# Message passing on a graph: more rows fetched by SyncE, and gates by tanh in PSUM

## The chip, the cores and the metric

The kernel runs on one core of one Trainium2 chip. The metric is the device time of one execution in microseconds. The core has five engines with queues of their own: TensorE (PE; its weight loads are listed as PEld), VectorE (DVE), ScalarE (ACT), GpSimd (POOL) and SyncE (SP), which computes nothing and issues DMAs. "PEq", "SPq" and so on are the sequencers, where waits and DMA issues happen.

## What is computed

One layer of an equivariant graph network, with a residual and a layer norm. There are 12500 nodes with 160 features each (64 scalars and 32 vectors of 3) and 400000 edges, sorted by their destination `dst`; `src` is random. Cut to what matters:

```python
h   = lin1(x) * a                                   # per node: 64 scalars, 32 x 3
w   = silu(edge_scalars @ fc_w1) @ fc_w2            # per edge: 224 weights
es, ev = h_s[src], h_v[src]                         # the gather: one row of 160 per edge
mid = products of w, es, ev and edge_attr           # per edge
agg = segment_sum(mid, dst) / 4                     # per node
pre = (self connection of x + agg @ lin2) * a       # 96 scalars, 32 x 3
y   = concat(silu(pre_s[:64]), sigmoid(pre_s[64:96])[:, None] * pre_v)
out = layernorm(x + y)
```

The node attribute `a` scales `pre` as a whole, so silu(z) = z * sigmoid(z) with z = a * pre, and the vectors' gate is sigmoid(a * pre_s[64:96]).

## The kernel before, in words

**Prologue** (lines 203 to 413). The node table `h_tab` (12500 rows of 160 floats, 640 bytes) is made and written to HBM. Weights, indices and constants are loaded. `at` holds the node attribute by tile of 128 nodes.

**Steps** (lines 862 to 908). The edges are cut into 3125 tiles of 128. A step takes a *quad*, four tiles; there are 782 steps. The order of all engines' instructions is written out by hand (`tc.manual_schedule`): each engine runs its instructions in the order in which this loop emits them. Step n emits:

- `fetch(n + 4)`: DMAs on SyncE, the `es` chunk (the edge scalars, two DMAs of 384 KB, once in six steps, two buffers; L200) and indices and edge attributes (L156, L157).
- `fetch_rows(n)` (L735 to L746): see below.
- the gather (L452 to L459): one indirect DMA on GpSimd per tile into `hg`, four buffers of a quad each; or, if the quad is one of `own`, the buffer `hq` that SyncE has filled.
- `weights` (L490): four matmuls from `hid` into `pw` in PSUM, two buffers.
- `turning.pop(0)()`: a tile of nodes, if one is due; what it returns runs on VectorE after the first product (`first`, L884).
- `one_hot` (L561), `products` (L508, and L516 three times) and `select_quad` (L570) on VectorE.
- `add`s into the node sums `acc` (L609), then a later stage of a node job (`step_on`).
- `sum_up`: for the quad two steps back, matmuls `sel`^T x `pr` into `pa` (L577), and when a block is complete its copy on ScalarE (L790).
- `hide(n + 2)`: once in two steps, the hidden layer (L447 on TensorE, Silu on ScalarE, L449), from `es`.
- `output`, `turn_blocks`: the maps of sixteen finished blocks (L601) and the transposes of one pair of blocks (L586). They, the hidden layer, the self connection (L770) and the node tiles share two PSUM banks, `misc`, in turn.

**Rows by SyncE.** `own` (L461) is every 68th step from 76 on that holds a whole quad: 11 quads. For the quad of step m, `places` (L465) loads its 512 indices, at step m-74; `tensor_scalar_mul` on VectorE (L741) turns them to byte offsets at step m-66, two steps behind the own quad before. The fetch is cut into 32 jobs of 16 rows (L479 to L486): one register load of 16 offsets (L480), and 16 DMAs of 640 bytes (L485). A job is emitted on each step whose number is even. The buffer `hq` is single, and SyncE's queue runs in order: its `es` loads, index loads, node loads `xt` (L625) and output stores (L677) stand between the jobs.

**Node jobs** (`finish`, L612 to L680). When the sums of four tiles of 128 nodes are complete, a job is begun (`begin`, L852): its `xt` rows are loaded, and its stages follow one per step. Four `turn`s: two transposes of `acc` into a `misc` bank (L636), which VectorE scales by `at` into `z` (L637). Then `gates`: one Sigmoid over the four tiles on ScalarE (L643). `gated`: two products per tile (L648, L649). `residual`: the addition of `xt` (L657). `moments` (L662, L664), `root` (Sqrt on ScalarE, L668), `norm` (L672, L674) and the store of the output by SyncE (L677). The last job, four tiles of which one is part filled, runs all its stages behind the last step; there `spans` lets each product take all four tiles at once.

Of the kernel before, what the change touches and what calls it, by code (L numbers as in the profile page):

```python
# [10 lines left out]
F32 = mybir.dt.float32  # L11
# [4 lines left out]
AF = mybir.ActivationFunctionType  # L16
OP = mybir.AluOpType
# [4 lines left out]
P = 128  # L22
S = 64
V = 32
V3 = 3 * V
D = S + V3
# [9 lines left out]
CT = 2 * SIDE  # L36
AHEAD = 3 * CT
NF = 4
OWN = 68
BATCH = 16  # L40
EVERY = 2

MARGIN = 128
NO = 16
# [13 lines left out]
def gnn_kernel(  # L58
# [21 lines left out]
    nc = tc.nc  # L80
    N = x.shape[0]
    NT = attr.shape[1]
# [8 lines left out]
    consts = ctx.enter_context(tc.tile_pool(name="consts", bufs=1))  # L91
# [100 lines left out]
    def load_chunk(c, queue=nc.sync):  # L192
        if c in ess:
            return
        t0, halves = chunks[c]
        es = ess[c] = loads.tile([2 * S, SIDE * P], F32, name="es")
        for half, n in enumerate(halves):
            to = es[half * S:(half + 1) * S]
            e0 = (t0 + half * halves[0]) * P
            queue.dma_start(to[:, :n * P], es_t[:, e0:e0 + n * P])  # L200


    ident = consts.tile([P, P], F32, name="ident")
# [24 lines left out]
    with tc.tile_pool(name="nodes", bufs=len(starts)) as nodes, tc.tile_pool(  # L228
        name="nodes_ps", bufs=6, space=PSUM
# [22 lines left out]
        at = consts.tile([P, NT], F32, name="at")  # L252
# [60 lines left out]
        for c0, cn, quarters, cq, xa, xz in loaded:  # L313
# [3 lines left out]
            nt = -(-cn // P)  # L317
            first = c0 // P
            full = cn // P
            for t0 in range(0, nt, U):  # L320
                ps = nps.tile([P, U, P], F32, name="hp")
                for t in range(t0, min(t0 + U, nt)):
                    n = min(P, cn - t * P)
                    nc.tensor.matmul(ps[:n, t - t0], xa[:, t * P:t * P + n], l1,
                                     start=True, stop=True)
                k = min(U, full - t0)
# [3 lines left out]
                if t0 + k < nt <= t0 + U:  # L330
                    n = cn - full * P
# [6 lines left out]
            for u in range(-(-cq // P)):  # L338
                n = min(P, cq - u * P)
# [10 lines left out]
            if cn > full * P:  # L350
                n = cn - full * P
# [7 lines left out]

    load_chunk(0, nc.gpsimd)  # L360
    nc.gpsimd.dma_start(dt, dst)
    iota = consts.tile([P, W], F32, name="iota")
    nc.vector.tensor_copy(iota, iota_i)
    for half in range(2):
# [22 lines left out]
    for to, part, pieces, w, r0, c0, by in maps:  # L387
        for k, piece in enumerate(pieces):
# [3 lines left out]
            m = terms.setdefault((to, part, four), len(terms))  # L392
# [20 lines left out]
    acc = sums.tile([V3, 2, NP], F32, name="acc")  # L413
# [46 lines left out]

    own = [n for n in range(OWN + 8, len(steps) - 4, OWN) if len(steps[n][2]) == Q]  # L461
    by_bytes = h_tab.rearrange("n d -> (n d)").bitcast(U8)
    row_bytes = 4 * D

    def places(pool, n):  # L465

        at_bytes = pool.tile([Q, P], I32, name="at_bytes")
        for k, (t, _, _) in enumerate(steps[n][2]):
            g, u = divmod(t, GT)
            with nc.allow_non_contiguous_dma(reason="the indices of one tile"):  # L470
                nc.sync.dma_start(at_bytes[k:k + 1], src[g][:, u:u + 1].rearrange("p u -> u p"))
        return at_bytes

    def rows_of(pool, at_bytes):

        hq = pool.tile([P, Q, D], F32, name="hq", bufs=1)
        flat_hq = hq.rearrange("p t d -> p (t d)").bitcast(U8)

        def job(t, p0):  # L479
            _, values = nc.values_load_multi_w_load_instructions(  # L480
                at_bytes[t:t + 1, p0:p0 + BATCH], engines=[ENG.SP], min_val=0,
                max_val=(N - 1) * row_bytes,
                skip_runtime_bounds_check_because="every entry of src is the index of a node")
            for p, v in enumerate(values, p0):
                nc.sync.dma_start(flat_hq[p:p + 1, t * row_bytes:(t + 1) * row_bytes],  # L485
                                  by_bytes[ds(v, row_bytes)][None])  # L486

        return hq, [lambda t=t, p0=p0: job(t, p0) for t in range(Q) for p0 in range(0, P, BATCH)]
# [123 lines left out]
    def finish(fin, psum, t0, nt, p, most=NF):  # L612


        whole = nt if p == P else nt - 1
        spans = [(0, nt)] if t0 + nt == tiles_of_nodes else [(k, k + 1) for k in range(nt)]
        xt = fin.tile([P, most, D], F32, name="xt", bufs=2)
        held = []
        if whole < nt:
            nc.vector.memset(xt[:, whole], 0.0)  # L620
        parts = [(slice(t0 * P, (t0 + whole) * P), slice(0, whole), P)] if whole else []
        if whole < nt:
            parts.append((slice((t0 + whole) * P, (t0 + whole) * P + p), slice(whole, nt), p))
        for nodes_of, k, n in parts:
            nc.sync.dma_start(xt[:n, k], x[nodes_of, :].rearrange("(t p) d -> p t d", p=n))  # L625

        def turn(k):
            if not held:
                held.extend(fin.tile([P, most, *shape], F32, name=name) for name, shape in (
                    ("z", [2 * V3]), ("sg", [V3]), ("y", [D]), ("st", [6]), ("mv", [2]),  # L630
                    ("rs", [])))
            z = held[0]
            c = (t0 + k) * P
            pp = psum.tile([P, 2, V3], F32, name="pp", tag="misc")
            for m in range(2):
                nc.tensor.transpose(pp[:, m], acc[:, m, c:c + P], ident[:V3, :V3])  # L636
            return lambda: nc.vector.tensor_scalar(  # L637
                z[:, k], pp.rearrange("p m c -> p (m c)"), at[:, t0 + k:t0 + k + 1], None,
                op0=OP.mult)

        def gates():
            z, sg = held[:2]
            nc.scalar.activation(sg[:, :nt], z[:, :nt, :V3], AF.Sigmoid)  # L643

        def gated():
            z, sg, y = held[:3]
            for k, m in spans:
                nc.vector.tensor_mul(y[:, k:m, :S], z[:, k:m, :S], sg[:, k:m, :S])  # L648
                nc.vector.tensor_mul(  # L649
                    y[:, k:m, S:].rearrange("p t (c i) -> p t i c", i=3),  # L650
                    z[:, k:m, V3:].rearrange("p t (i c) -> p t i c", i=3),
                    sg[:, k:m, None, S:].to_broadcast([P, m - k, 3, V]))

        def residual():
            y = held[2]
            for k, m in spans:
                nc.vector.tensor_add(y[:, k:m], y[:, k:m], xt[:, k:m])  # L657

        def moments():
            _, _, y, st, mv, _ = held  # L660
            for k in range(nt):
                nc.vector.bn_stats(st[:, k], y[:, k])  # L662
            for k in range(nt):
                nc.vector.bn_aggr(mv[:, k], st[:, k])  # L664

        def root():
            mv, rs = held[4:]
            nc.scalar.activation(rs[:, :nt], mv[:, :nt, 1], AF.Sqrt, bias=eps)  # L668

        def norm():  # L670
            _, _, y, _, mv, rs = held
            nc.vector.reciprocal(rs[:, :nt], rs[:, :nt])  # L672
            for k in range(nt):
                nc.vector.tensor_scalar(y[:, k], y[:, k], mv[:, k, 0:1], rs[:, k:k + 1],  # L674
                                        op0=OP.subtract, op1=OP.mult)
            for nodes_of, k, n in parts:
                nc.sync.dma_start(out[nodes_of, :].rearrange("(t p) d -> p t d", p=n), y[:n, k])  # L677

        return [lambda k=k: turn(k) for k in range(nt)] + [
            gates, gated, residual, moments, root, norm]  # L680


    tiles_of_nodes = -(-N // P)
# [5 lines left out]
    with tc.tile_pool(  # L689
        name="fin", bufs=1  # L690
    ) as fin, tc.tile_pool(
        name="mine", bufs=2
    ) as mine, tc.tile_pool(
        name="late", bufs=2
    ) as late, tc.tile_pool(name="edge", bufs=2) as edge, tc.tile_pool(
        name="deep", bufs=4
# [36 lines left out]
        at_of, hq_of, rows_due = {}, {}, []  # L733

        def fetch_rows(n):  # L735

            for m in own:
                if n == max(1, m - OWN - 6):
                    at_of[m] = places(mine, m)
                if n == m - OWN + 2:  # L740
                    nc.vector.tensor_scalar_mul(at_of[m], at_of[m], float(row_bytes))  # L741
                    hq_of[m], jobs = rows_of(mine, at_of[m])
                    rows_due.extend((m, job) for job in jobs)
            if n % EVERY == 0 and rows_due:
                rows_due.pop(0)[1]()
            assert all(m > n for m, _ in rows_due)  # L746

# [114 lines left out]
        with tc.manual_schedule(engines={ENG.PE, ENG.DVE, ENG.Activation, ENG.Pool, ENG.SP}):  # L862
# [6 lines left out]
            for n, (c, i, tiles) in enumerate(steps):  # L869
# [3 lines left out]
                if n in checks:  # L873
                    checks[n]()
                fetch(n + 4)
                fetch_rows(n)
                hg = hq_of.pop(n) if n in own else gather(deep, [index(t) for t, _, _ in tiles])
                pw = weights(pw_ps, hids[c, i // 2], [(half, u - i // 2 * 4) for _, half, u in tiles])
# [62 lines left out]
        with tc.For_i(0, n_redo, 1):  # L941
# [9 lines left out]
            with tc.For_i(0, n_again, 1) as g, tc.For_i(0, GT, 1) as k:  # L951
                t = g * GT + k
# [12 lines left out]
                for k, op in enumerate((OP.min, OP.max)):  # L965
# [14 lines left out]
                                        op1=OP.mult)  # L980
# [69 lines left out]
```

## Time and profile before

| what | value |
|---|---|
| median of 10 runs | 3971.7 us (3969.57 to 3973.46) |
| profiled execution | 3970.37 us |
| its span | 3968.4 us |
| mean granted TensorE clock | 0.971 |
| gathers on GpSimd | 3081 |
| row fetches on SyncE | 5632 |
| Silu, Sigmoid and Sqrt table loads on ScalarE | 48, 25, 25, of 1.283 us each |
| DMA traffic | 412.51 MB, mean 104 GB/s |

The profile is of one execution. A line of its groups gives source line, engine, operation, "out<-in" by the program's names, shapes and count; then busy time and the mean of one in ns; then the idle time of the engine just before them, and what ended most of it. "issue" means that the engine waited for nothing that the profile shows. In a list of waits, a line reads: who waited, for what, total us, times, longest. A timeline lists start, duration, engine, line, operation and count, with adjoining instructions merged. A line of one source line's instructions gives count, minimum, median and maximum in ns, and the first and last start in us. Instructions of SyncE are never counted as busy; its queue is seen in timelines and waits alone.

### The profile page before, as it was taken

How to read it: one execution, taken by the hardware profiler on the slowest of the kernel's cores; microseconds unless marked ns; L12 is line 12 of the kernel's file. 1: busy time of each engine (PE TensorE's matmuls, PEld its weight loads, DVE VectorE, ACT ScalarE, POOL GpSimd, SP SyncE). 2: the span in 40 equal slices, each digit the busy share in tenths (PEclk: the TensorE clock that was granted, in tenths of full speed). 3: DMA queues.
4: the chain of work that ended last, by engine and by line, in shares of the span. 5: the costliest groups of instructions: out<-in, count | busy, mean ns of one | idle time of the engine just before them, and what ended most of it. 6: DMA issues, size and time to landing. Idle time of an engine off the chain costs nothing. (4 is left out here: it accounts for less than half of the span.)

```text
span 3968.4 us, 58310 instructions
## 1 busy us (share of the span) xinstructions
PE 3649.9 (92%) x14291; PEld 1585.7 (40%) x14291; DVE 2416.6 (61%) x6607; ACT 939.9 (24%) x2463; POOL 2946.3 (74%) x3100
## 2 busy tenths in 40 slices
PE   5999999998999999999999999999999999999997
PEld 4343343343444344334334344344343344343343
DVE  5656665655665665656656556656665665665665
ACT  1322221221222222212212222222222222222222
POOL 4777777777777777777777777777777777777774
PEclk8999999999999999999999999999999999999998
DMA  8343444344434344343443433433434444334332
GB/s 231 96 107 86 109 102 105 98 103 105 100 98 109 96 102 105 101 109 89 107 112 90 105 99 99 108 99 96 111 99 107 99 103 105 98 99 108 99 95 67
DMA packets 243271, 412.51 MB, mean 104 GB/s; under 512 B 83147, under 2 KB 173575, under 8 KB 242023
## 3 DMA queue, kind: packets, MB, share of 16 engines
q0 software_dynamic: 150160, 262.93, 25.4%
q1 hardware_dynamic: 92246, 145.66, 15.5%
q8 instruction: 115, 1.88, 0.2%
q14 instruction: 236, 1.93, 0.2%
q10 hardware_dynamic: 514, 0.10, 0.0%
HBM read 392.43 MB, written 16.00 MB: 103 GB/s over the span
## 5 line engine op out<-in xcount | busy, mean ns | idle before, releaser
L456 POOL DMA_INDIRECT hg<-h_tab,idx x3081 | 2932.1, 952 | 946.0 <-issue 850.9
L498 PE MATMUL pw<-w,hid 128*128 128x448 f32 x3126 | 1368.1, 561 | 168.6 <-DVE sel L570 127.6
L577 PE MATMUL pa<-pr,sel 128*64 128x416 f32 x6250 | 1291.8, 535 | 0.0
L516 DVE TENSOR_TENSOR pr<-pw,hg 128x384 f32<-128x384 f32 x2313 | 1137.8, 548 | 0.0
L508 DVE TENSOR_TENSOR pr<-pw,hg 128x512 f32<-128x512 f32 x771 | 532.9, 691 | 933.3 <-DMA hg<-h_tab,idx 669.7
L498 PEld LDWEIGHTS pw<-w,hid 128*128 128x128 f32 x3126 | 555.2, 194 | 649.5 <-issue 453.1
L577 PEld LDWEIGHTS pa<-pr,sel 128*64 128x64 f32 x6250 | 385.9, 138 | 806.1 <-issue 795.3
L790 ACT COPY sa<-pa 128x416 f32<-128x416 f32 x521 | 263.1, 505 | 1366.5 <-PE pa L577 1361.3
L561 DVE TENSOR_TENSOR pw<-rel,iota 128x64 f32<-128x64 int16 x782 | 179.8, 230 | 511.0 <-PE pw L498 506.8
L447 PE MATMUL misc<-es,w 128*128 128x512 f32 (+1 forms) x784 | 445.2, 650 | 22.4 <-DMA es<-in_es_t_dram 19.6
L449 ACT ACTIVATE hid<-misc 128x512 f32<-128x512 f32 x392 | 233.5, 596 | 714.8 <-PE misc L447 714.3
L586 PEld LDWEIGHTS misc<-ident,sa 128*128 128x128 f32 x2084 | 239.5, 141 | 332.5 <-issue 250.7
L601 PE MATMUL misc<-tt,l 128*96 128x256 f32 (+5 forms) x1496 | 349.0, 381 | 13.5 <-DVE z L637 12.0
L586 PE MATMUL misc<-ident,sa 128*128 128x128 f32 x2084 | 329.6, 281 | 20.5 <-DVE z L637 10.6
L570 DVE TENSOR_TENSOR sel<-pw,eas 128x256 f32<-128x256 f32 x782 | 324.4, 415 | 0.0
L589 ACT COPY tt<-misc 128x192 f32<-128x192 f32 x521 | 164.6, 316 | 537.3 <-PE misc L586 522.8
L601 PEld LDWEIGHTS misc<-tt,l 128*96 128x96 f32 (+1 forms) x1496 | 229.0, 164 | 151.8 <-issue 73.0
L447 PEld LDWEIGHTS misc<-es,w 128*128 128x128 f32 x784 | 118.5, 190 | 283.9 <-issue 224.6
L609 DVE TENSOR_TENSOR acc<-acc,os 96x32 f32 x1042 | 195.2, 187 | 23.8 <-ACT os L604 5.5
L591 ACT COPY tt<-misc 128x64 f32<-128x64 f32 x521 | 117.1, 225 | 0.0
L604 ACT COPY os<-misc 96x512 f32<-96x512 f32 (+2 forms) x68 | 38.3, 563 | 316.6 <-PE misc L601 309.2
L636 PE MATMUL misc<-ident,acc 96*128 96x96 f32 x196 | 35.1, 264 | 49.3 <-DVE pw L561 30.8
(87 smaller groups left out, 680.6 us busy)
## 6 DMA issues: line engine op xcount, KB each, us to landing
es<-in_es_t_dram SPq DMA_DIRECT2D x258, 384.0 KB
hq<-h_tab SPq DMA_DIRECT2D x5632, 0.6 KB
hg<-h_tab,idx POOLq DMA_INDIRECT x3081
h_tab<-ht POOLq DMA_DIRECT2D x6, 1280.0 KB
xt<-in_x_dram SPq DMA_DIRECT2D x23, 320.0 KB
out_dram<-y SPq DMA_DIRECT2D x23, 320.0 KB
xv<-in_xv_t_dram SPq DMA_DIRECT2D x25, 187.5 KB
xs<-in_xs_t_dram SPq DMA_DIRECT2D x25, 125.0 KB
```

Of the source, the lines that this page charges most:

```text
L447: nc.tensor.matmul(ph[:k, c], w1[:k, :k], es[:k, t0 * P + c0 * P:t0 * P + c1 * P], start=True, stop=True)
L449: nc.scalar.activation(hid[:k, c], ph[:k, c], AF.Silu, scale=1.0 / math.sqrt(64))
L456: nc.gpsimd.indirect_dma_start(out=hg[:, t, :], out_offset=None, in_=h_tab, in_offset=bass.IndirectOffsetOnAxis(ap=i, axis=0))
L498: nc.tensor.matmul(pw[:, t:t + m, :NWT], hid[:m * S, c * P:(c + 1) * P], w2[:m * S, :m], start=True, stop=True)
L508: nc.vector.tensor_mul(two, pw[:, :n, :2 * S].rearrange("p t (k c) -> p t k c", k=2), hg[:, :n, None, :S].to_broadcast([P, n, 2, S]))
L516: nc.vector.tensor_mul(pr[:, :n, first:first + V3].rearrange("p t (i c) -> p t i c", i=3), pw[:, :n, None, 2 * S + k * V:2 * S + (k + 1) * ...
L570: nc.vector.tensor_mul(sel[:, :n], oh[:, :, None, :].to_broadcast([P, n, 4, W]), by_slot(tiles[0][0])[:, u:u + n, :, None].to_broadcast([P ...
L577: nc.tensor.matmul(pa[half * ROWS:(half + 1) * ROWS, :NPR], sel[:, t].rearrange("p k w -> p (k w)"), pr, start=start, stop=stop)
L586: nc.tensor.transpose(pt[:, four * P:four * P + k], sa[:k, c:c + P], ident[:k, :k])
L601: nc.tensor.matmul(po[:, k, :nb], l2[r, terms[to, part, four]], a[:, :nb], start=(n == 0), stop=(n == len(of) - 1))
L609: nc.vector.tensor_add(window, window, os[:, :, b])
L790: nc.scalar.copy(sa, pas.pop(j)[:, :NPR])
```

## The change

Three constants and the node jobs are changed.

- `OWN` is 48 instead of 68, so `own` is steps 56, 104, ... 776: 16 quads. `places` comes at step m-54 and the scaling at step m-46, still two steps behind the own quad before.
- A job of 16 rows is emitted on the steps whose number is not a multiple of 4, three of four, instead of on every second.
- The gates use sigmoid(z) = (1 + tanh(z/2)) / 2. A constant `half_at` holds at/2. In `turn`, the two transposes go to one stretch of a `misc` bank; ScalarE takes tanh of the scalars' half from PSUM, scaled by `half_at`, into `g`. The function that runs after the first product is three VectorE instructions per tile: (g + 1) * pre for the 64 scalars and for the 96 vector components, both from PSUM into free columns of the same bank, and that times `half_at` plus `xt` into `y`. The stages `gates`, `gated` and `residual`, the tiles `z` and `sg`, and `spans` go. A job has four `turn`s, `moments`, `root` and `norm`: seven steps instead of ten.

```diff
-OWN = 68
+OWN = 48
 BATCH = 16
-EVERY = 2
+EVERY = 4
...
+    half_at = consts.tile([P, NT], F32, name="half_at")
+    nc.vector.tensor_scalar_mul(half_at, at, 0.5)
...
-            z = held[0]
+            g, y = held[:2]
             c = (t0 + k) * P
-            pp = psum.tile([P, 2, V3], F32, name="pp", tag="misc")
+            pp = psum.tile([P, 512], F32, name="pp", tag="misc")
             for m in range(2):
-                nc.tensor.transpose(pp[:, m], acc[:, m, c:c + P], ident[:V3, :V3])
-            return lambda: nc.vector.tensor_scalar(
-                z[:, k], pp.rearrange("p m c -> p (m c)"), at[:, t0 + k:t0 + k + 1], None,
-                op0=OP.mult)
-
-        def gates():
...
-        def gated():
...
-        def residual():
...
+                nc.tensor.transpose(pp[:, m * V3:(m + 1) * V3], acc[:, m, c:c + P], ident[:V3, :V3])
+            half = half_at[:, t0 + k:t0 + k + 1]
+            nc.scalar.activation(g[:, k], pp[:, :V3], AF.Tanh, scale=half)
+            pg = pp[:, 2 * V3:2 * V3 + D]
+
+            def gate():
+                nc.vector.scalar_tensor_tensor(pg[:, :S], g[:, k, :S], 1.0, pp[:, :S],
+                                               op0=OP.add, op1=OP.mult)
+                nc.vector.scalar_tensor_tensor(
+                    pg[:, S:].rearrange("p (c i) -> p i c", i=3),
+                    g[:, k, None, S:].to_broadcast([P, 3, V]), 1.0,
+                    pp[:, V3:2 * V3].rearrange("p (i c) -> p i c", i=3),
+                    op0=OP.add, op1=OP.mult)
+                nc.vector.scalar_tensor_tensor(y[:, k], pg, half, xt[:, k],
+                                               op0=OP.mult, op1=OP.add)
+
+            return gate
...
         return [lambda k=k: turn(k) for k in range(nt)] + [
-            gates, gated, residual, moments, root, norm]
+            moments, root, norm]
...
-            if n % EVERY == 0 and rows_due:
+            if n % EVERY and rows_due:
                 rows_due.pop(0)[1]()
```

More of the change, by code (lines that the diff above doesn't have):

```diff
@@ L615, in finish @@
         whole = nt if p == P else nt - 1
-        spans = [(0, nt)] if t0 + nt == tiles_of_nodes else [(k, k + 1) for k in range(nt)]
         xt = fin.tile([P, most, D], F32, name="xt", bufs=2)
@@ L629, in turn @@
                 held.extend(fin.tile([P, most, *shape], F32, name=name) for name, shape in (
-                    ("z", [2 * V3]), ("sg", [V3]), ("y", [D]), ("st", [6]), ("mv", [2]),
-                    ("rs", [])))
-            z = held[0]
+                    ("g", [V3]), ("y", [D]), ("st", [6]), ("mv", [2]), ("rs", [])))
+            g, y = held[:2]
             c = (t0 + k) * P
-            pp = psum.tile([P, 2, V3], F32, name="pp", tag="misc")
+            pp = psum.tile([P, 512], F32, name="pp", tag="misc")
@@ L635, in turn @@
             for m in range(2):
-                nc.tensor.transpose(pp[:, m], acc[:, m, c:c + P], ident[:V3, :V3])
-            return lambda: nc.vector.tensor_scalar(
-                z[:, k], pp.rearrange("p m c -> p (m c)"), at[:, t0 + k:t0 + k + 1], None,
-                op0=OP.mult)
-        def gates():
-            z, sg = held[:2]
-            nc.scalar.activation(sg[:, :nt], z[:, :nt, :V3], AF.Sigmoid)
-        def gated():
[L646 to L652, printed above, removed]
@@ L654, in residual @@
-        def residual():
-            y = held[2]
-            for k, m in spans:
-                nc.vector.tensor_add(y[:, k:m], y[:, k:m], xt[:, k:m])
+                nc.tensor.transpose(pp[:, m * V3:(m + 1) * V3], acc[:, m, c:c + P], ident[:V3, :V3])
[12 more added lines that the diff above has]
+                                               op0=OP.mult, op1=OP.add)
@@ L659, in moments @@
+            return gate
         def moments():
-            _, _, y, st, mv, _ = held
+            _, y, st, mv, _ = held
             for k in range(nt):
@@ L666, in root @@
         def root():
-            mv, rs = held[4:]
+            mv, rs = held[3:]
             nc.scalar.activation(rs[:, :nt], mv[:, :nt, 1], AF.Sqrt, bias=eps)
         def norm():
-            _, _, y, _, mv, rs = held
+            _, y, _, mv, rs = held
             nc.vector.reciprocal(rs[:, :nt], rs[:, :nt])
```

## The prediction

> **What bounds the kernel now.** I read the page first, then the list of waits, then the timeline of GpSimd, and last the timeline and the waits of SyncE's queue. The page:
>
> ```profile
> PE 3649.9 (92%) x14291; PEld 1585.7 (40%) x14291; DVE 2416.6 (61%) x6607; ACT 939.9 (24%) x2463; POOL 2946.3 (74%) x3100
> L456 POOL DMA_INDIRECT hg<-h_tab,idx x3081 | 2932.1, 952 | 946.0 <-issue 850.9
> L508 DVE TENSOR_TENSOR pr<-pw,hg 128x512 f32<-128x512 f32 x771 | 532.9, 691 | 933.3 <-DMA hg<-h_tab,idx 669.7
> ```
>
> TensorE shows the largest share, but the second line decides. A gather takes 0.952 us, and 850.9 us of the 946.0 us of idle time ahead of gathers is "issue": nothing held them. The third line shows the first product of each step waiting 669.7 us for the gathered rows. GpSimd's timeline, first and last gather:
>
> ```profile
> 61.44 1.04 POOL L456 DMA_INDIRECT hg<-h_tab,idx  x1 [7.28 <-issue]
> ...
> 3931.31 0.95 POOL L456 DMA_INDIRECT hg<-h_tab,idx  x1 [0.31 <-issue]
> ```
>
> From 61.44 to 3932.26 us there are 3081 gathers, 1.256 us each, without a hole. Nearly all else is slack: GpSimd sets the pace, 4 x 1.253 = 5.01 us per step of four tiles. A quad that SyncE fetches spares GpSimd four gathers. That is why SyncE's queue is the second thing to read. Its instructions are not counted as busy on the page, so its load has to be taken from its own rows.
>
> ```profile
> L480 SPq TENSOR_LOAD <-at_bytes x352: 982/1232/1893, 117.0 to 3785.2; - x176
> L485 SPq DMA_DIRECT2D hq<-h_tab x5632: 219/228/312, 118.3 to 3792.5; - x195
> ```
>
> ```profile
> 2309.42 0.41 SPq L677 DMA_DIRECT2D out_dram<-y  x1
> 2309.93 1.13 SPq L200 DMA_DIRECT2D es<-in_es_t_dram  x2
> 2312.63 20.75 SPq L485 DMA_DIRECT2D hq<-h_tab  x48
> 2333.48 1.11 SPq L200 DMA_DIRECT2D es<-in_es_t_dram  x2
> 2336.16 19.73 SPq L485 DMA_DIRECT2D hq<-h_tab  x48
> ```
>
> ```profile
> SPq L677 <- DVE pw L561: 60.8, 2, 35.0
> SPq L485 <- DMA es<-in_es_t_dram: 14.6, 12, 1.9
> ```
>
> The second fence is the timeline of SyncE's queue: three batches of 16 rows take about 20 us, and one `es` load with three batches 23.5 us (2309.93 to 2333.48). The third is what that queue waited for from 2142 to 2458 us, the window in which the quad of step 484 is fetched. It waited 60.8 us at two output stores (it had run ahead of VectorE) and 14.6 us behind `es` transfers: a row's DMA is held until the load ahead of it has drained.
>
> **The SyncE part, step by step.** Before, own quads are steps 76, 144, ... 756: 11. After, 56, 104, ... 776: 16. So 5 x 4 = 20 gathers go, 20 x 1.256 = 25.1 us of GpSimd, and 2560 row fetches come.
>
> *What a fetch costs SyncE.* A batch alone is one register load, 1.23 us and its gap, and 16 rows in 5.12 us: 6.45 us, 206 us for the 32 of a quad. Top down, with everything that the queue carries: from the first load at about 2142.2 to the last row at 2457.9 us is 315.7 us; less the 60.8 us at output stores and 2.1 us of waits for a free `es` buffer leaves 252.8 us of work. This covers 62 steps with ten pairs of `es` loads. After, the 32 batches lie in 42 steps (three of four, from step m-46 to m-5, for own step m), with seven pairs. Three pairs at 1.27 us of issue and some 1.5 us of wait go, 8.3 us, and a third of the index, edge and node transfers, 3 us. So W = 252.8 - 8.3 - 3 = 241.5 us.
>
> *When it may begin and must end.* The first register load waits for VectorE's scaling of the indices (L741), which stands two steps behind the last own quad; the buffer `hq` is single. VectorE's timeline around step 416 prices this:
>
> ```profile
> 2135.01 0.69 DVE L508 TENSOR_TENSOR pr<-pw,hq 128x512 f32<-128x512 f32 x1
> 2139.14 0.69 DVE L508 TENSOR_TENSOR pr<-pw,hg 128x512 f32<-128x512 f32 x1
> 2141.79 0.29 DVE L741 TENSOR_SCALAR at_bytes<-at_bytes 4x128 int32<-4x128 int32 x1
> ```
>
> From the own quad's product to the scaling is 6.8 us. Then 0.3 us to the load, W, and about 2 us until the last rows are there (the shortest time from a gather's end to the product that uses it is 1.7 us; I found no row for a single row's landing). GpSimd's cycle for 48 steps is 47 x 5.01 = 235.6 us; SyncE's is 6.8 + 0.3 + 241.5 + 2 = 250.6 us. SyncE is 15 us too slow, and **it becomes the bound**. Before, the same two sums were 67 x 5.01 = 336 us for GpSimd and 262 us for SyncE.
>
> *What is queued behind it.* SyncE runs behind the steps inside a window, so the output stores no longer hold it (the 60.8 us vanish because they were slack), but the `es` loads come late: in order behind the batches, they feed TensorE's L447. The last load of a window is issued at step m-6, followed by two batches and the index loads, 16 us, and 2 us of landing: the rows are there 18 us after it. The load itself takes about 6 us (the batch held behind it starts again 5 to 6 us after it) and 1.1 us of matmul, and then come some 3.5 steps at the 4.0 us that steps 416 to 421 took when nothing held them (2135.01 to 2155.03 for five), 14 us, and 2 us to the product: 23 us. So up to 5 us more; bounds 0 (if TensorE catches up faster) and 7. I take 5: a cycle of 255.6 us.
>
> *A page that speaks otherwise.* The row says 1.232 us for a register load. The Trainium skill, "DMA: Bandwidth & Descriptors", section "Latency and other measured facts", puts the floor of such a load at about 600 ns. By it W would be 20 us less, the cycle 235 us, and the time GpSimd's own, about 3945 us; the row decides, since no load in the trace is under 0.98 us.
>
> **The gates.** Per tile, the scaling from PSUM (408 ns, L637), two products (215 and 281 ns) and the residual (316 ns) go, 1.22 us, and three instructions with a PSUM operand come. The trace has none of that kind; from the PSUM products of 384 and 512 columns (547, 691 ns) they would take 0.71 us in all, by three times the scaling's row 1.22 us. VectorE gains 0 to 0.5 us a tile, 0 to 50 us over 98 tiles; it has 39% idle, so I count nothing. ScalarE gets 98 tanh of 225 to 316 ns (L591, L589) for 25 sigmoids of 523 ns. Table loads are 1.283 us; 25 for sigmoid go; tanh needs none if it lies in Silu's table, and up to 98, with Silu's reloads, if it does not. ScalarE is 76% idle; at worst the gate, and the products queued behind it, wait 1.28 us in 98 steps, 126 us that lie beside SyncE's longer work. The misc bank is held until the third instruction, about 0.7 us longer; TensorE now waits 58 us behind L637, and that may grow by half, unseen. The residual now needs `xt` one step after its load is issued, not six: VectorE waits there for SyncE to come up, but SyncE's own work is no longer for it, so I count 0, with 8 us x 24 jobs as the other end. Behind the last step the four scalings, gate, products and residual last from 3948.25 to 3952.49 us; four tiles of three instructions take about as long: 0, give or take 1 us.
>
> **The sum.** First register load at 117.0 us as now; first own product at 117 + 241.5 + 2 + 5 = 365.5; fifteen cycles of 255.6, 3834, bring step 776 to 4199.5. Before, from the last own product (3815.0 us, step 756) to the end of the span is 153.4 us; with 20 fewer steps of 5.0 us, 53.4. Span 4253; the profiled execution took 3970.4 for a span of 3968.4, so 2 more: **4255 us**. Its sum is against 3970.4, which lies 1.3 us under the median of 3971.7.
>
> **Rivals.**
> - *GpSimd stays the bound* (ends on the other side). Decided at W = 226.5 us, where SyncE's cycle is 235.6. For it: 206 us of bare batches, 9 of bare `es` issues and some 11 of the other transfers come to 226 us. Against it: the 14.6 us behind `es` in one window. Price: 3970.4 - 25.1 = 3945 us. Chance 0.1, and 0.02 for a cycle that lands within 0.2% of now.
> - *SyncE bounds, but holds behind `es` and late `es` cost nothing*, since compute waits in any case: cycle 255.6 - 10.5 - 5 = 240 to 245, 4005 to 4085. Chance 0.18.
> - *SyncE bounds as summed*, cycle 249 to 261: 4150 to 4340. Chance 0.62.
> - *The gates add to it*: `xt` late by 8 us in 24 jobs, or table loads that lengthen the stretch from own quad to scaling: 4255 + 190 = 4445. Chance 0.08.
>
> That the change does not take effect is excluded: steps and batches follow from the constants. The range leaves out the first and last: 4040 to 4345. A difference of 0.2% (8 us) is about what can be told here: faster 0.1, same 0.02, slower 0.88.
>
> **What would show it.** Right: GpSimd's gathers show waits of several us before step 104 and every 48th step; the product at own steps waits for `hq`; SyncE's waits at L677 shrink to a few us; L447 waits for `es`. Wrong: gathers at 1.253 us without a hole, rows of the last batch landed before their step, or a window's W below 230 us.

## The result and the profile after

The changed kernel takes **4281.12 us** (median of 8 runs, 4274.31 to 4285.45) against 3970.71 us for the kernel before (28 runs beside it): a ratio of 1.078 [1.077, 1.0789], 7.8% slower. The forecast was 4255 us, its range 4040 to 4345. The profiled execution has a span of 4276.3 us at a mean granted TensorE clock of 0.934 (before 3968.4 at 0.971). Line numbers of the kernel after lie a little lower or higher: the gather is L458, SyncE's register load L482, its row DMA L487, the hidden matmul L449, the gates L638 to L649, the output store L672, the scaling of the indices L736.

The page of the kernel after, first the busy times, then three of its groups:

```profile
PE 3718.4 (87%) x14291; PEld 1635.5 (38%) x14291; DVE 2442.9 (57%) x6524; ACT 899.5 (21%) x2488; POOL 2910.4 (68%) x3080
L458 POOL DMA_INDIRECT hg<-h_tab,idx x3061 | 2896.1, 946 | 1278.7 <-issue 849.4
L449 PE MATMUL misc<-es,w 128*128 128x512 f32 (+1 forms) x784 | 494.4, 716 | 398.6 <-DMA es<-in_es_t_dram 373.4
L510 DVE TENSOR_TENSOR pr<-pw,hg 128x512 f32<-128x512 f32 x766 | 529.1, 691 | 158.0 <-DMA hg<-h_tab,idx 100.9
```

Every engine's share has fallen: the bound is none of the five that the page counts as busy. GpSimd did 20 gathers fewer, 25 us, but its idle time ahead of gathers rose from 946.0 to 1278.7 us while "issue" stayed at 849.4. The first product now waits 100.9 us for gathered rows instead of 669.7: the gathers are no longer late. TensorE, which waited little for `es`, waits 373.4 us. The kernel after in the list of waits:

```profile
PE misc L449 <- DMA es<-in_es_t_dram: 373.4, 76, 13.1
POOL hg L458 <- DMA hq<-h_tab: 198.9, 31, 12.8
POOL hg L458 <- DVE pr L518: 136.6, 84, 5.8
DVE y L649 <- DMA xt<-in_x_dram: 103.6, 15, 10.9
```

and what SyncE's own queue waited for:

```profile
SPq L482 <- DVE pw L563: 210.9, 14, 18.9
SPq L487 <- DMA es<-in_es_t_dram: 124.2, 121, 2.1
SPq L672 <- DVE y L669: 29.5, 1, 29.5
```

Everything that waits in the first list waits for a load of SyncE's queue or for a product (L518). The queue itself (second list) waits for VectorE for long only between windows (L482, the first register load, 14 times); a *window* is the stretch from the first register load of an own quad to its last row. Its waits at the output store are one of 29.5 us and one of 18.2, both behind the last window; before they were 556.3 us in 21. The line that puts 198.9 us on `hq` names the wrong load. A gather does not read `hq`, and 33 of the 93 holes in GpSimd's work (212 of the 340 us by which they exceed the usual 0.3 us between gathers) end at a semaphore whose last DMA was an index load. Such a place, in the timelines of SyncE and of GpSimd:

```profile
2344.82 10.51 SPq L487 DMA_DIRECT2D hq<-h_tab  x29
2355.43 1.12 SPq L200 DMA_DIRECT2D es<-in_es_t_dram  x2
2356.86 0.37 SPq L156 DMA_DIRECT2D idx<-in_src_dram  x1
```

```profile
2353.48 0.94 POOL L458 DMA_INDIRECT hg<-h_tab,idx  x1 [0.30 <-issue]
2362.49 0.94 POOL L458 DMA_INDIRECT hg<-h_tab,idx  x1 [8.07 <-DMA hq<-h_tab]
```

GpSimd stands still for 8.07 us until the index load issued at 2356.86 us has landed. That load stood behind rows. And the end of a window, step 440, in the timelines of SyncE and VectorE:

```profile
2395.01 10.42 SPq L487 DMA_DIRECT2D hq<-h_tab  x28
2405.52 1.15 SPq L200 DMA_DIRECT2D es<-in_es_t_dram  x2
```

```profile
2413.95 0.23 DVE L563 TENSOR_TENSOR pw<-rel,iota 128x64 f32<-128x64 int16 x1 [0.83 <-PE pw L500]
...
2417.61 0.69 DVE L510 TENSOR_TENSOR pr<-pw,hq 128x512 f32<-128x512 f32 x1 [0.17 <-DVE pw L563]
...
2424.74 0.21 DVE L736 TENSOR_SCALAR at_bytes<-at_bytes 4x128 int32<-4x128 int32 x1
```

The last row goes out at 2405.4 us, the own quad's product starts 12.2 us later, and 7.1 us after that start the scaling lets the next window begin. The product waited for the weights `pw` (TensorE), not for `hq`; in no window of this run does an own quad's first product wait for `hq`.

The SyncE part of the span, by the prediction's own terms (from the rows of VectorE and SyncE; means over the windows):

| term | predicted | measured |
|---|---|---|
| first own product | 365.5 | 360.4 |
| own product to scaling, and to the first load | 6.8 + 0.3 | 7.1 + 0.3 |
| W, SyncE's work in a window | 241.5 | 239.7 (237.9 to 242.4) |
| last row to own product | 2 + 5 | 9.9 (5.5 to 13.7) |
| cycle of 48 steps | 255.6 | 257.3 |
| last own product to the end of the span | 53.4 | 56.5 |
| span | 4253 | 360.4 + 15 x 257.3 + 56.5 = 4276 |

### The profile page after: what moved, and what is told of

Its sections match the earlier page's. It is cut to its first block, busy times and chain, and to the rows that moved or that the text cites. A ratio compares the mean times of both kernels' runs of the same rounds, so it can differ in the third digit from the quotient of the medians.

```text
span 4276.3 us, 63629 instructions
## 1 busy us (share of the span) xinstructions
PE 3718.4 (87%) x14291; PEld 1635.5 (38%) x14291; DVE 2442.9 (57%) x6524; ACT 899.5 (21%) x2488; POOL 2910.4 (68%) x3080
## 5 line engine op out<-in xcount | busy, mean ns | idle before, releaser
L458 POOL DMA_INDIRECT hg<-h_tab,idx x3061 | 2896.1, 946 | 1278.7 <-issue 849.4
L518 DVE TENSOR_TENSOR pr<-pw,hg 128x384 f32<-128x384 f32 x2298 | 1130.2, 547 | 0.0
L563 DVE TENSOR_TENSOR pw<-rel,iota 128x64 f32<-128x64 int16 x782 | 183.2, 234 | 1445.1 <-PE pw L500 1444.2
L449 PE MATMUL misc<-es,w 128*128 128x512 f32 (+1 forms) x784 | 494.4, 716 | 398.6 <-DMA es<-in_es_t_dram 373.4
L500 PEld LDWEIGHTS pw<-w,hid 128*128 128x128 f32 x3126 | 569.3, 198 | 495.3 <-issue 464.8
L510 DVE TENSOR_TENSOR pr<-pw,hg 128x512 f32<-128x512 f32 x766 | 529.1, 691 | 158.0 <-DMA hg<-h_tab,idx 100.9
L603 PE MATMUL misc<-tt,l 128*96 128x256 f32 (+5 forms) x1496 | 384.2, 409 | 1.5 <-ACT tt L593 1.5
L449 PEld LDWEIGHTS misc<-es,w 128*128 128x128 f32 x784 | 128.3, 205 | 660.7 <-issue 577.2
L603 PEld LDWEIGHTS misc<-tt,l 128*96 128x96 f32 (+1 forms) x1496 | 253.5, 180 | 164.1 <-issue 92.7
L611 DVE TENSOR_TENSOR acc<-acc,os 96x32 f32 x1042 | 194.4, 187 | 25.1 <-ACT os L606 6.9
L649 DVE SCALAR_TENSOR_TENSOR y<-misc,half_at,xt 128x160 f32<-128x160 f32 x98 | 37.6, 384 | 106.5 <-DMA xt<-in_x_dram 103.6
```

The costliest lines, as they stand in the source:

```text
L449: nc.tensor.matmul(ph[:k, c], w1[:k, :k], es[:k, t0 * P + c0 * P:t0 * P + c1 * P], start=True, stop=True)
L458: nc.gpsimd.indirect_dma_start(out=hg[:, t, :], out_offset=None, in_=h_tab, in_offset=bass.IndirectOffsetOnAxis(ap=i, axis=0))
L500: nc.tensor.matmul(pw[:, t:t + m, :NWT], hid[:m * S, c * P:(c + 1) * P], w2[:m * S, :m], start=True, stop=True)
L510: nc.vector.tensor_mul(two, pw[:, :n, :2 * S].rearrange("p t (k c) -> p t k c", k=2), hg[:, :n, None, :S].to_broadcast([P, n, 2, S]))
L518: nc.vector.tensor_mul(pr[:, :n, first:first + V3].rearrange("p t (i c) -> p t i c", i=3), pw[:, :n, None, 2 * S + k * V:2 * S + (k + 1) * ...
L603: nc.tensor.matmul(po[:, k, :nb], l2[r, terms[to, part, four]], a[:, :nb], start=(n == 0), stop=(n == len(of) - 1))
```

## The experiments

Seven runs, e1 to h1, told in a group at the end, were made where the kernel before itself took 5250 to 5340 us; the others were made where it took 3972 to 3975 us, as for the result. A ratio is always to runs of the kernel before at the same place and time, and what the two kinds of places give is not mixed.

**k1: the changed kernel as it is**, beside the next one.

> The changed kernel itself, unaltered, as the control for the kernels beside it. On a chip where the kernel before takes 3971 us: 4281 again, ratio 1.078. On one where it takes 5300 us: SyncE's work per window was 353 us there with the old gates (6185 us, ratio 1.163); the same within 1%, ratio 1.155 to 1.175 (theory A; the gates add at most the 0.3% that they cost alone). Rival B would have it 0.02 or more above the 1.163 of the constants alone.

4282.24 us against 3971.88, 1.078 [1.0762, 1.0798], as expected; W 237.8 to 241.9 us. It stands for the changed kernel in what follows.

**m1: the gates alone.** The constants are those of before, the gates and node jobs those of after.

```diff
-OWN = 48
+OWN = 68
-EVERY = 4
+EVERY = 2
-            if n % EVERY and rows_due:
+            if n % EVERY == 0 and rows_due:
```

> The changed kernel with the two constants put back: the gates alone, on a chip where the kernel before takes 3972 and the changed one 4282 us. Theory A: GpSimd stays the bound with 3081 gathers; VectorE's and ScalarE's savings lie beside it: 3971 us, give or take 5 (1.003 was measured where all queues ran slowly). Rival B (the wait for xt, 103.6 us in the changed kernel, and the bank held longer cost time by themselves): 4030 us or more, with holes between gathers.

3961.71 us (3957.99 to 3964.05) against 3975.47: 0.9966 [0.9954, 0.9978]. The expected 3971, give or take 5, was missed: the gates, which I had counted at nothing, make the kernel 13.8 us *faster*, and the loss of the change lies in its constants: 4281 - 3962, some 320 us. (The constants alone were not run where the kernel before takes 3972 us; this is a difference.) Where the 13.8 us come from is seen in the rows of the gathers from 400 to 3900 us, first of before, then of m1:

```profile
L456 POOL DMA_INDIRECT hg<-h_tab,idx x2787: 942/946/2307, 399.5 to 3900.0; - x200
```

```profile
L458 POOL DMA_INDIRECT hg<-h_tab,idx x2798: 942/946/1098, 399.5 to 3899.6; - x200
```

The median is the same, 946 ns, but the longest was 2307 ns and is 1098. Before, 25 gathers took over 1.1 us, 14.8 us in excess of 946 ns each; in m1 three do, 0.9 us, all in the prologue. Of the 25, four lie in the prologue and 21 lie beside L648, L649 or L657, the products and the residual of a node job. GpSimd's and VectorE's timelines of before:

```profile
2129.57 1.80 POOL L456 DMA_INDIRECT hg<-h_tab,idx  x1 [0.30 <-issue]
...
2134.18 1.61 POOL L456 DMA_INDIRECT hg<-h_tab,idx  x1 [0.30 <-issue]
```

```profile
2129.57 0.21 DVE L648 TENSOR_TENSOR y<-z,sg 128x64 f32<-128x64 f32 x1
2129.70 0.28 DVE L649 TENSOR_TENSOR y<-z,sg 128x96 f32<-128x96 f32 x1
...
2133.81 1.02 DVE L657 TENSOR_TENSOR y<-y,xt 128x160 f32<-128x160 f32 x4
```

The gather that begins amid the run of products takes 1.80 us, the one that begins amid the four additions 1.61 us. These VectorE instructions read both operands from SBUF. In m1 one operand of each lies in PSUM, and no gather that begins beside them is stretched. The products of the steps (L508, L516) have one operand in PSUM as well, and gathers beside them take 0.95 us. The additions into `acc` (L611 in m1), 187 ns each with both operands in SBUF, are still there: of 124 gathers that begin while one runs, 16 take 50 to 152 ns longer. This is what the Trainium skill, "SBUF — State Buffer", section "Who interferes with whom", states: a VectorE instruction with two SBUF inputs contends with a GpSimd instruction that reads SBUF. The page has no price for a gather; here the excess is 0.2 to 1.4 us for each of the 21. The profiled executions differ by 12.4 us of span: 14.7 us less in gathers and 0.7 us ahead of the first, against 3.1 us more behind the last (39.2 us in place of 36.1).

What the gates cost by themselves, from the groups of the kernel after, kept apart by shape:

```profile
L638 ACT ACTIVATE g<-misc,half_at 128x96 f32<-128x96 f32 x98 | 33.4, 341 | 180.0 <-PE misc L636 176.5 <-PE pw L500 3.5
L451 ACT ACT_TABLE_LOAD x25 | 32.1, 1283 | 58.6 <-DMA dt<-in_dst_dram 31.9 <-PE misc L449 26.4
L642 DVE SCALAR_TENSOR_TENSOR misc<-g,misc 128x64 f32<-128x64 f32 x98 | 21.7, 221 | 3.0 <-ACT g L638 2.8
L644 DVE SCALAR_TENSOR_TENSOR misc<-g,misc 128x96 f32<-128x96 f32 x98 | 25.7, 262 | 3.3
L649 DVE SCALAR_TENSOR_TENSOR y<-misc,half_at,xt 128x160 f32<-128x160 f32 x98 | 37.6, 384 | 106.5 <-DMA xt<-in_x_dram 103.6
```

Three instructions of 221, 262 and 384 ns take 0.87 us per tile in place of 1.22. No table is loaded ahead of tanh (L638 has none): 25 loads ahead of Silu and 25 ahead of Sqrt are left of 98.

**m2: `es` earlier.** The changed kernel with the `es` chunk looked up six steps ahead instead of four; nothing else moves.

```diff
+            if n + 2 < len(steps) and steps[n + 2][1] == 0:
+                load_chunk(steps[n + 2][0])
...
-                if i == 0:
-                    load_chunk(c)
```

> The changed kernel with each es chunk's loads issued two steps earlier in SyncE's queue, the same work on every queue. Theory A with the late es as the last stretch of the cycle: in the changed kernel 9.8 us pass from the last row issued to the own quad's product, because TensorE waits for es (373.4 us in all) and has 3 to 4 steps to do after it; with es early the rows are last, 2 us: cycle 257 - 7 = 250 us, 4282 - 16 x 7 = 4170 us, and the wait for es falls under 100 us. If the late es is no more than a symptom of SyncE's load: 4282 within 15.

4193.58 us against 3975.47, 1.0546 [1.053, 1.0562], near the expected 4170: of the 310 us lost, some 90 come back. W stays at 241.7 us. From the last row to the own product it takes 2.4 us (mean; 9.9 in the changed kernel), and the cycle is 251.5. 16 windows x 5.8 us are 93 us. Its list of waits:

```profile
PE misc L449 <- DMA es<-in_es_t_dram: 76.4, 20, 12.1
POOL hg L458 <- DMA idx<-in_src_dram: 112.8, 23, 13.6
DVE y L649 <- DMA xt<-in_x_dram: 210.9, 15, 20.3
```

TensorE's wait for `es` falls from 373.4 to 76.4 us. The wait for `xt` doubles, and the kernel is faster all the same: that wait is hidden in the time that SyncE needs anyway. So the 2 us of landing were right, and the late `es` made 7.5 us of the stretch from the last row to the own product, where 5 was taken. The cycle gains only 5.8 of them, since W is 2 us longer (the rows wait 161.2 us behind `es` loads in place of 124.2). W bounds what is left.

**k2: 32 rows per job**, in three of eight steps, so that a register load fetches 32 offsets.

```diff
-BATCH = 16
+BATCH = 32
-            if n % EVERY and rows_due:
+            if 3 * n % 8 < 3 and rows_due:
```

> The changed kernel with jobs of 32 rows in place of 16, three of them in eight steps in place of three in four: the same 512 row DMAs per own quad at the same mean density, but one register load where there were two? If a load of 32 registers is one instruction of 1.23 us, 16 loads and their gaps go, 16 x 1.28 = 20 us of SyncE's 240 per window: cycle 237, next to GpSimd's 235.6, 3960 to 4010 us where the kernel before takes 3971 (ratio 1.00 to 1.01). If the load's time goes by registers: 4281 within 30. On a slow chip (353 us per window) the same 20 us of some 377: 5% less than the changed kernel beside it.

4169.34 us against 3971.88, 1.0498 [1.0481, 1.0516]. The expected 3960 to 4010 was missed. SyncE's register load in the kernel after, then in k2 (shortest, median, longest in ns):

```profile
L482 SPq TENSOR_LOAD <-at_bytes x512: 983/1232/2432, 115.8 to 4200.7; - x171
```

```profile
L482 SPq TENSOR_LOAD <-at_bytes x256: 1874/2126/3394, 116.0 to 4084.2; - x128
```

The load is not a fixed cost: twice the registers take 2.126 instead of 1.232 us, 56 ns for each further one. A window saves 32 x 1.232 - 16 x 2.126 = 5.4 us of loads and 1.5 us of gaps around them, and the rows wait 52.7 us behind `es` loads in place of 124.2, 4.5 us less a window. W, without waits at output stores, is 227.5 us, 12 less. In seven of the 16 windows the queue also waits some 11 us at an output store, so the mean cycle is 250.4. This fits W as the bound: a shorter W gives a shorter cycle, and GpSimd's 235.6 is still not reached.

**m3: all of it together**, with a little less for SyncE: 32 rows a job, `es` early, `OWN` 50, node jobs three steps later so that `xt` has time.

```diff
-OWN = 48
-BATCH = 16
+OWN = 50
+BATCH = 32
...
-            if n % EVERY and rows_due:
+            if 3 * n % 8 < 3 and rows_due:
...
-                    turning.extend(job[:nt])
+                    turning.extend([lambda: (lambda: None)] * 3 + job[:nt])
```

> A version made to fit SyncE: own quad every 50th step (15 quads), jobs of 32 rows, three in eight steps (a load of 32 registers took 2.13 us, so a window is 228 us of work), es issued two steps earlier, and a node job's first turn three steps after its xt is issued; the new gates. Theory A: SyncE's cycle is 7.1 + 0.3 + 229 + 2 = 238 us, GpSimd's 49 x 5.01 = 245.5 us: GpSimd is the bound with 3065 gathers, 16 fewer than before, 3972 - 20 = 3952 us, faster than both. If SyncE's queue still holds it by more than the sum says: 3970 to 4020. Rival B: 4050 or more.

4050.31 us against 3975.47, 1.0189 [1.0175, 1.0203]: missed by a hundred. The number lies at the edge of what rival B expected, but m1 has shown that the gates alone cost nothing. W came down to 227 us as expected, yet the cycle is 253 (242 to 260), not GpSimd's 49 x 5.01 = 245.5. The last row goes out 6 to 25 us before the own product, so SyncE no longer ends last. Its waits:

```profile
PE misc L449 <- DMA es<-in_es_t_dram: 79.9, 22, 14.4
POOL hg L458 <- DMA idx<-in_src_dram: 50.1, 12, 9.6
```

GpSimd has 29 holes, 114 us: 7.6 us a cycle, which is the difference. Some 50 of it are index loads that stand in SyncE's queue; the rest ends at VectorE's instructions, products above all. What makes those late is not settled: TensorE still waits 80 us for `es`, and I ran no version with the index loads on earlier steps.

GpSimd's ledger closes over all of these. m1's profiled 3958 us, less 1.25 us for each gather that goes, plus the holes in GpSimd's work, plus the change of the tail behind the last gather: for the changed kernel 3958 - 25 + 340 + 8 = 4281 (profiled 4278); m2 3958 - 25 + 249 + 7 = 4189 (4192); k2 3958 - 25 + 230 + 5 = 4168 (4166); m3 3958 - 20 + 114 - 1 = 4051 (4055).

**The runs at the other places.** There even the unchanged kernel needs a third longer. m1's kernel ran at both kinds. Its `MOVE` between two row DMAs on SyncE, first at such a place (e2), then where the kernel before takes 3975 us (m1):

```profile
L487 SPq MOVE hq<-h_tab x5632: 2/29/1409, 142.3 to 5103.5; - x195
```

```profile
L487 SPq MOVE hq<-h_tab x5632: 29/29/42, 117.2 to 3768.2; - x195
```

An instruction that takes 29 to 42 ns takes up to 1409 ns there, though it waits for nothing. In such stretches SyncE advances by one or two instructions per 0.70 us; from 1500.88 us on in e2, eight rows take 10 us. Other engines stand still in waits that the profile puts down to nothing on the core (`remote`: 1350.3 us for VectorE at L563 in e2, none in m1). That instructions reach the engines late is my reading of it; no run proves it. Nor is it shown that the chip makes the difference: the record has chip number 1 for f5 and h1, where the kernel before took 5338 and 5324 us, and again, an hour after h1, for m1 to m3, where it took 3975.

*e1, the constants alone* (kernel before with `OWN` 48, `EVERY` 4 and the new test), and *e2, the gates alone* (m1's kernel):

> The kernel before with the two constants alone: own step every 48, jobs on three of four steps; gates as before. Theory A (SyncE's queue is the bound: cycle = 7.1 own to scaling + 0.3 + 240 of work + 9.8 from the last row issued to the product = 257 us per 48 steps): 4270 to 4290 us, within 15 us of the changed kernel's 4281. Rival B (the gates make a good part of the loss, by xt waited for one step after its issue, 103.6 us at the third gate instruction, and the bank held for longer): 4281 less 60 to 190, 4090 to 4220 us. A expects the output stores not to hold SyncE here either.

> The changed kernel with the two constants put back (own step every 68, jobs on even steps): the gates alone. Theory A: GpSimd stays the bound, 3081 gathers at 1.256 us without a hole; VectorE's and ScalarE's savings lie beside it: 3971 us, give or take 5. Rival B (the wait for xt and the bank held longer cost time by themselves): 4030 us or more, with holes between gathers. A third reading, that fewer stages shorten the way behind the last step: 3 to 6 us faster.

e1: 6185.51 against 5324.99, 1.1628 [1.1568, 1.1688]. e2: 5332.7, 1.003 [1.0005, 1.0056]. There too the constants alone lose and the gates alone do not; the changed kernel itself was not run there. The gates' gain isn't seen there. GpSimd does not run without holes: its gathers wait 1303.7 us for products in e2.

*e3, the `es` loads issued by ScalarE*:

```diff
-                    load_chunk(c)
+                    load_chunk(c, nc.scalar)
```

> The changed kernel with the es loads issued from ScalarE's queue in place of SyncE's; all else the same. SyncE loses seven pairs of issues per window, 9 us of its 240. Theory A with the hold behind es a matter of queue order: another 10 us go, work per window 221 us, es comes in time, cycle 221 + 2 + 7.4 = 230 us, under GpSimd's 235.6: GpSimd is the bound again and the time is 3945 us, faster than both. Theory A with the hold a matter of the shared DMA engines (rows wait while 768 KB drain, whoever issues it): work 231, cycle 240.5, 4020 us. Rival B: no change beyond 20 us, 4260 or more, since the gates are untouched.

6979.74, 1.3129 [1.306, 1.3198]: a miss by all three theories. Rows on SyncE's queue still wait for `es` loads, though another queue issues them, and far longer. SyncE's waits, first of e1, then of e3:

```profile
SPq L485 <- DMA es<-in_es_t_dram: 60.8, 73, 1.8
```

```profile
SPq L487 <- DMA es<-in_es_t_dram: 747.6, 74, 36.3
```

The trace shows why. The DMAs of SyncE and of ScalarE share eight completion semaphores, numbered 100 and 102 to 108, which the program gives out in turn, and each DMA first waits until the one that had its semaphore before has landed. In the kernel before, a row eight DMAs behind an `es` load therefore waits for that load. In e3 the semaphore can belong to an `es` load that ScalarE has not yet issued. The longest wait is such a place: the row is due at 1455.71 us and waits for semaphore 102, ScalarE comes to the load of that semaphore 32 us later, and the row goes at 1492.06, 4.2 us after the issue.

```profile
1487.81 1.12 ACTq L200 DMA_DIRECT2D es<-in_es_t_dram  x2
```

The hold is thus made by the program's semaphores, and neither theory of it (queue order, shared DMA engines) names them. Whether `es` on another queue would pay with semaphores of its own was not tried, nor was the edit where the kernel before takes 3972 us.

*e4, `es` early* (m2's kernel), *e5, `OWN` 56*, and *f5, `OWN` 56 with the jobs in five of eight steps* (`n % 8 < 5`):

> The changed kernel with each es chunk's loads issued two steps earlier in SyncE's queue (same work on every queue). Theory A: TensorE's wait for es (373.4 us in the changed kernel) goes for the most part, and at the end of a window the rows themselves are last, 2 us behind the last issue in place of 9.8: cycle 250 us, 4281 - 15 x 7.5 = 4165 us. If the late es is no more than a symptom (the step's own work after the last row takes these 9.8 us anyway): 4281 within 15. Rival B: no change, 4281.

> The changed kernel with an own quad on every 56th step in place of every 48th (13 quads, the jobs still on three of four steps, the new gates). Theory A in its numbers of a chip on which the kernel before takes 3971 us: SyncE's cycle grows by eight steps of other transfers, 257 + 6 = 263 us, GpSimd's by eight steps to 55 x 5.01 = 275.6 us, so GpSimd is the bound again and two quads fewer are gathered than before: 3971 - 10 = 3961 us, without holes between the gathers. If some other thing in the change costs the time (rival B, the gates; or the denser jobs as such, by late es loads): 4050 us or more.

> The changed kernel with an own quad on every 56th step and the jobs spread evenly over the window: five steps of eight (in place of three of four). Theory A: what counts is SyncE's load per step while jobs are on it. By the profile of the changed kernel: 5 x 6.6 us of jobs, 4 us of es loads with their holds and 2 us of the rest in eight steps, 39 us against GpSimd's 8 x 5.01 = 40; the late es loads go, GpSimd is the bound, and two quads fewer are gathered than before: 3961 us where the kernel before takes 3971, a ratio of 0.997. On a chip where SyncE is slower (5978 us for 56 steps with three of four, ratio 1.138): between 1.0 and 1.138, nearer to 1.08, as the own step's cycle loses the free steps at its end. Rival B (the gates): no better than with three of four.

e4: 6218.3 against 5324.99, 1.1689 [1.1626, 1.1752]. e5: 5978.68 against 5253.57, 1.1376 [1.1353, 1.1399]. f5: 5795.21 against 5338.46, 1.0836 [1.0796, 1.0876]. e4 gains nothing over e1 there: the stretch from the last row to the own product falls from 12.0 to 2.0 us, but W grows from 354 to 369. e5's expected gain was missed; f5 came out as expected, near 1.08. With the same number of rows, spreading the jobs over more steps is worth five points: in e5 the last row goes out some 65 us before its product, so the steps first run at SyncE's pace and then, with nothing left to fetch, at their own.

*h1, one DMA of 16 fixed rows in place of a job's 16 row DMAs* (own quads then get the wrong rows; the register loads stay):

```diff
-            for p, v in enumerate(values, p0):
-                nc.sync.dma_start(flat_hq[p:p + 1, t * row_bytes:(t + 1) * row_bytes],
-                                  by_bytes[ds(v, row_bytes)][None])
+            nc.sync.dma_start(hq[p0:p0 + BATCH, t], h_tab[p0:p0 + BATCH, :])
```

> The changed kernel with each job's sixteen row DMAs replaced by one DMA of sixteen fixed rows of the table (the own quads get other nodes' rows, so their messages are left out; same number of own quads, same register loads, same bytes). SyncE's work per window falls from 240 us to some 32 x 1.9 + 30 = 90 us; gathers, gates, node jobs and all waits on them stay. Theory A: GpSimd is the bound, 3061 gathers without a hole: 3945 us where the kernel before takes 3971, ratio 0.993. Rival B (the gates, the wait for xt, the bank held longer): still 4150 us or more. On a chip where SyncE's queue runs slowly (the kernel before takes 5300 us there, its work 410 us a window): theory A expects that with SyncE's load gone most of that goes too, 4000 to 4400 us, ratio 0.75 to 0.83; if those chips are slow for another reason, 5200 us or more.

5145.84 against 5324.08, 0.9665 [0.9605, 0.9725]. With the instructions of the rows gone, what the change loses is gone and 3.35% is won, so the loss is in the many small row DMAs on SyncE. (The edit also takes away the scattered addresses, and does not tell the instructions from the transfers.) But the kernel does not come near 4000 us: the rest of the program is slow there as well.

## Why the prediction was right, and where its sizes were off

1. *SyncE becomes the bound.* Right. k2, which changes nothing but SyncE's jobs, takes 113 us off the changed kernel; 16 windows x 7 us of cycle are 112. m1 shows that the other half of the change does not lose.
2. *W = 241.5 us.* Measured 239.7, in m2 241.7. The top-down sum (the queue's own window less its waits, then less what three `es` pairs and a third of the small loads take) held to 2 us. It rests on one window; the same sum over the eleven windows of before gives 249 to 261 us, 254 in the mean, where this one gave 252.8. The register load is 1.232 us at the median and no shorter than 0.983 in the kernel after. The floor of about 600 ns that the prediction set against it from the Trainium skill ("DMA: Bandwidth & Descriptors", section "Latency and other measured facts") is not contradicted by this: a floor is no price for 16 registers, and k2 shows that the price grows with their number. The hold of rows behind `es` loads, 1.5 us a pair in the sum, was there; e3 shows that the program's semaphores make it.
3. *What begins a window*: 6.8 + 0.3, measured 7.1 + 0.3.
4. *The last row to the own product, 2 + 5*: 9.9 measured, and what the own product waits for last is `pw`, not `hq` as I had named it. This is the mis-sized term of the SyncE part. m2 tells its halves apart: landing 2.4, late `es` 7.5, where 5 was taken and 7 was the bound. That the cycle was only 1.7 us short is in part luck: 2.9 us too little here, 1.8 too much in W. 15 x 1.7 us of cycle make 26 us; with the first window (-5) and the tail (+3) this is the 23 us between 4255 and the profiled 4278.
5. *The gates count nothing.* In the sum of the changed kernel this held: W is SyncE's. By themselves they are worth -13.8 us (m1). Behind the last step, where 0 give or take 1 was said, they cost 3.1 us. The step priced VectorE's time (0.35 us a tile, within the 0 to 0.5 given) and the table loads (48 fewer, the good end), and left out what VectorE's instructions do to GpSimd's. The clue stood in the profile of before: the gathers' mean of 0.952 us against 0.946 for most of them, over 3081 gathers 18 us.
6. *`xt` one step after its load*: VectorE waits 103.6 us in 15 waits, unseen behind SyncE, as counted; m2's 210.9 us confirm that it is hidden.
7. *The index loads* were only counted as work in W. They came late too (212 us of GpSimd's holes). In the changed kernel I take that for the same lateness seen on another engine; in m3 some 50 us of holes are left of it. No version had them earlier.

The rival in which holds and late `es` cost nothing had a cycle of 240 to 245 us: the late `es` did cost, by m2, and the holds stand in W (124.2 us in all). GpSimd stayed the bound in none of the versions with 48 steps. No version that fetches more rows one by one by SyncE beat the kernel before; the best one found is m1, the new gates with the old constants, 0.9966 [0.9954, 0.9978].

## What to carry to other kernels

An engine that only issues DMAs has no busy time on the page; before moving work to it, sum its instructions over one period of the schedule, with everything else that stands in its queue, and compare that with the period that the other engines would need. What stands in the same queue behind the moved work (here `es` and index loads) comes late by as much, and issuing it some steps earlier is a cheap remedy (m2: some 90 us of 310). Before a load is moved to another queue, see which semaphores its DMAs share with those of the first (e3). A mean a little above the median in the bounding engine's row is worth a look at the longest instances and what runs beside them.

## What the runs showed of the hardware that was not expected

- The products and additions of the node jobs (L648, L649, L657), with both operands in SBUF, stretched 21 gathers from 0.946 to as much as 2.307 us; the same work with one operand in PSUM stretched none (m1).
- A register load on SyncE takes 1.232 us for 16 registers and 2.126 us for 32.
- None of 98 tanh needed a table load beside Silu.
- The same kernel took 3962 us in m1 and 5333 us in e2, at a granted clock of 0.969 and 0.862; what makes the difference is open.
